# Two outlook-attention layers: the second layer's writes move to GpSimd's queue, its last softmax multiply to VectorE

## The chip, the cores and the metric

The kernel runs on one core of one Trainium2 chip. The time is the device time of one execution in microseconds, the median of three runs. A core has five engines with an instruction queue each, which run side by side and wait for one another through semaphores: TensorE (PE in the profile, its weight loads PEld), VectorE (DVE), ScalarE (ACT), GpSimd (POOL) and SyncE (SP, which only issues transfers). [...] An instruction that starts a transfer stands in its engine's queue like any other: if it has to wait for its data, what stands behind it waits too. Transfers of all queues are carried out by the same 16 DMA engines of the core.

## What is computed

The input is eight images of 56 x 56 pixels with 384 channels, in float32. Two layers follow each other, each of the form x + layer(groupnorm(x)).

```python
# layer 0: outlook attention with 12 heads, 9 x 9 weights a pixel and head
v = einsum(x, Wv);  a = softmax(einsum(x, Wa).reshape(b, n, 12, 9, 9) * d ** -0.5)
out = einsum('bnhpq,bnqhd->bnphd', a, patches3x3(v))   # then overlap-added over 3 x 3
y = einsum(canvas, Wo)
# layer 1: 6 heads, 9 weights a pixel and head
a = softmax((x @ W_attn + b_attn).reshape(B, H * W, 6, 9))
v = x @ W_v + b_v
y = einsum('bpKhd,bphK->bphd', patches3x3(v), a)
return y.reshape(B, H, W, C) @ W_proj + b_proj
```

In layer 1 each pixel's result is, for each head, the sum of the 3 x 3 neighbouring v vectors, weighted by nine softmax weights; a projection and the residual follow. The change touches layer 1 alone.

## The kernel before

The images are taken in four pairs, and one image column of a pair is R = 112 rows (two images of 56). Layer 0 goes through the 56 columns of each pair and leaves x1, the input of layer 1, in DRAM. Layer 1 goes through 32 groups (NG) of PX = 7 columns: four pairs times eight groups. It is a software pipeline written out in the loop over `step` at the end of `layer1`, with seven steps a group; parts of group g-1 are done while group g's projections run. TensorE's instructions are kept in program order, and the pieces of contraction and output projection are laid between the projections by a list of jobs (`jobs.run`). The order on the other engines is set by a scheduler that plans the whole program when it is built.

The parts of a group, in the order in which data goes through them:

- `load` (L798): SyncE reads x1t, the group's input, 1176 KB. `normed` (L813): ScalarE writes the normalized xn, in pieces for each channel chunk and image.
- `attend` (L842 to L858): TensorE projects a tile of 128 pixels (`bank`, L119 in the profile, where all matmuls have the line of a helper). VectorE adds the biases: the logits lgt (L852), and v (L855, five buffers). The two `spread` calls, L317 in the profile, then write v to the table vtab in DRAM, with the columns that belong to two groups written twice. Seven of eight steps have such a tile, and each tile has two writes, of parts of two columns.
- `regroup`: lgt is written to lgtab by ScalarE's queue (L869), and SyncE reads it back as `at`, one row of pixels a partition (L877).
- `weigh` (L886 to L897): the softmax. VectorE takes the maximum (L891) and subtracts it (L892), ScalarE takes the exponential (L893), VectorE sums (L895) and takes the reciprocal (L896); then the nine weights are multiplied by that (L897).
- `move`: TensorE shifts the weights between rows (`pw`), ScalarE copies them into bands wz in nine pieces (L918) and writes these to the table ztab in DRAM (L920), 496 KB in pieces of 504 bytes.
- `fetch`: SyncE reads the v patches vp from vtab (L378, after the v that they need has landed), and the bands z from ztab (L329, after ztab has landed), four transfers a group. TensorE contracts z with vp (`pc`), ScalarE copies the result to yT (L956), TensorE projects it (`po`), VectorE adds bias and residual into x1t (L972).
- `turn`: TensorE transposes the result (`pt`, L122), ScalarE copies it to ot (L985), and at the end of each half of a group ot is written to the output (L987): 64 writes in all, 672 KB and 504 KB in turn.

So before the change three queues hold transfers or wait for them in layer 1: ScalarE's, with 392 writes of v (L317), lgtab (L869) and ztab (L920) between its copies, exponentials and normalizations; SyncE's, with all reads and the writes of results; and GpSimd's, which issues no transfer and only multiplies the weights (L897).

Of the kernel before, what the change touches and what calls it, by code (L numbers as in the profile page):

```python
# [10 lines left out]
ALU = mybir.AluOpType  # L11
# [4 lines left out]
def two_outlook_layers(  # L16
# [32 lines left out]
    nc = tc.nc  # L49

    B, H, W, C = x.shape
# [33 lines left out]
    PY1, NPY1, SX1, SY1 = 8, 7, PX + 2, 10  # L85
# [25 lines left out]
    vtab1 = dram.tile([NPX * (R + GAP) + GAP, SX1, C], F32, name="vtab1")  # L111
# [6 lines left out]
    def matmul(*args, **kwargs):  # L118
        tc.keep_in_program_order(nc.tensor.matmul(*args, **kwargs))  # L119
# [23 lines left out]
    def projected(name):  # L143
        return patch.tile([P, NCH, PX, IMG, H], F32, tag="yT", name=f"yT_{name}", bufs=1)
# [146 lines left out]
    def project(dst, lhs, w, lo, n):  # L291
        for i in range(NCH):
            matmul(
                dst, lhs[:, i], w[:, i, lo : lo + n], start=(i == 0), stop=(i == NCH - 1)
            )

    def patches_of(col, pad):

        for px in range(NPX):
            sx = col - PX * px + pad  # L300
            if 0 <= sx < PX + 2 * pad:
                yield px, sx

    def parts_of(tile_no):


        done = OVER * tile_no
        yield 0, tile_no, done, R - done
        yield R - done, tile_no + 1, 0, done + OVER

    def spread(queue, table, width, col, pad, row, v):

        (px, sx), *more = patches_of(col, pad)
        n, rows = 1 + len(more), v.shape[0]
        line = width * C
        first = (px * (R + GAP) + GAP + row) * line + sx * C
        queue.dma_start(  # L317
            bass.AP(
                table.tensor, table.offset + first,
                [[line, rows], [(R + GAP) * line - PX * C, n], [1, C]],  # L320
            ),
            v.unsqueeze(1).to_broadcast([rows, n, C]),
        )
# [35 lines left out]
    def bank(rows, lo, hi, of=NBANK):  # L359

        bank.turn = (bank.turn + 1) % of
        return banks[bank.turn][:rows, lo:hi]
# [10 lines left out]
    def patch_tiles(name, b):  # L373
        return patch.tile([P, NPY0, C], F32, tag="vp", name=f"vp_{name}_{b}")

    def rows_to_patches(vp, table, px, r0, py, npy, sx):
        first = (px * (R + GAP) + GAP - MARGIN + r0) * sx * C
        nc.sync.dma_start(  # L378
            vp,
            bass.AP(  # L380
                table.tensor, table.offset + first, [[C, vp.shape[0]], [py * sx * C, npy], [1, C]]
            ),
        )
# [400 lines left out]
    def layer1(pools, base, last_of_layer0, late_w):  # L784
# [57 lines left out]
        def attend(g, m):  # L842

            col = g * PX + m
            if col % SB == 0:
                return
            tile_no = col % SB - 1
            tokens = xns[col // SB % 2].rearrange("p i m r -> p i (m r)")
            tokens = tokens[:, :, tile_no * P : (tile_no + 1) * P]
            pa = bank(P, 0, NC1, 2)  # L850
            project(pa, tokens, wc_t, 0, NC1)
            nc.vector.tensor_add(staged[-1][1][:, len(staged[-1][0])], pa[:, :NA1], ba_t)  # L852
            staged[-1][0].append(col // SB * NT + tile_no)
            v = work.tile([P, C], F32, tag="v", name=f"v_1_{col}", bufs=5)
            nc.vector.tensor_add(v, pa[:, NA1:], bv_t)  # L855
            for lo, n_col, row, n in parts_of(tile_no):
                c = col - col % SB + n_col
                spread(nc.scalar, vtab1, SX1, c % W, 1, row, v[lo : lo + n])  # L858

        def stage(g):  # L860

# [24 lines left out]
        def weigh(g):  # L886

            at = lgs[g]
            heads_last = [R, PX, K2, HEADS1]
            mx = work.tile([R, PX, HEADS1], F32, tag="mx", name=f"mx1_{g}")  # L890
            nc.vector.tensor_reduce(mx, at.rearrange("r x k h -> r x h k"), AX.X, ALU.max)  # L891
            nc.vector.tensor_tensor(at, at, mx.unsqueeze(2).to_broadcast(heads_last), ALU.subtract)  # L892
            nc.scalar.activation(at, at, AF.Exp)  # L893
            den = work.tile([R, PX, HEADS1], F32, tag="den", name=f"den1_{g}")
            nc.vector.tensor_reduce(den, at.rearrange("r x k h -> r x h k"), AX.X, ALU.add)  # L895
            nc.vector.reciprocal(den, den)  # L896
            nc.gpsimd.tensor_tensor(at, at, den.unsqueeze(2).to_broadcast(heads_last), ALU.mult)  # L897

        def move(g):

# [27 lines left out]
        def fetch(g, due):  # L928
            pair, px = divmod(g, NPX)
            n_tile = 2  # L930
            yT = projected(f"1_{g}")
            x1t = x1ts.pop(g)
            vps = [patch_tiles(f"1_{g}", b)[: SX1 * SY1, :NPY1] for b in range(IMG)]
            for b in range(IMG):
                rows_to_patches(vps[b], vtab1, px, b * H + MARGIN - 1, PY1, NPY1, SX1)
            for b in range(IMG):
                z, vp = zs1[(g * IMG + b) % NZ], vps[b]
                bands(
                    nc.sync, z, ztab1[g % NTAB], LINE1, SLOT1, ROW1, MARGIN - 1, GROUPS1,
                    b, PY1, NPY1,  # L940
                )

                def contract(t, b=b, z=z, vp=vp):
                    lo, hi = t * n_tile, min(NPY1, (t + 1) * n_tile)
                    pc = ps.tile([P, NCH, n_tile, PY1, PX], F32, tag="c", name=f"pc1_{g}_{b}_{t}", bufs=NC)
                    for py in range(lo, hi):
                        zp = z[:, py].rearrange("s (y h m) -> s y h m", y=PY1, h=HEADS1)
                        for h in range(HEADS1):
                            i, j = divmod(h, P // D1)
                            matmul(  # L950
                                pc[j * D1 : (j + 1) * D1, i, py - lo],
                                vp[:, py, h * D1 : (h + 1) * D1],
                                zp[:, :, h, :],
                                start=True, stop=True,
                            )
                    nc.scalar.copy(  # L956
                        yT[:, :, :, b, lo * PY1 : hi * PY1],
                        pc[:, :, : hi - lo].rearrange("p i n y m -> p i m (n y)"),
                    )

                for t in range(0, (NPY1 + n_tile - 1) // n_tile, NC):
                    jobs.add(due, lambda t=t, f=contract: [f(t + n) for n in range(NC)])

                    jobs.add(due, turning.pop(0) if turning else lambda: None)

            def project_out(half, j):
                lo, hi = HALVES[half]
                n = (hi - lo) * R
                po = ps.tile([P, 4 * R], F32, tag="of"[(half * NCH + j) % 2], name=f"po1_{g}_{half}_{j}")
                project_half(po, wo_t, yT, half, j)  # L970
                res = x1t[:, j, lo:hi].rearrange("p m r -> p (m r)")
                nc.vector.scalar_tensor_tensor(  # L972
                    res, po[:, :n], bo_t[:, j : j + 1], res, ALU.add, ALU.add
                )

            def turn(m):

                half = m // 4
                lo, hi = HALVES[half]
                if m == lo:  # L980
                    fetch.ot = io.tile([R, 4, C], F32, tag="ot", name=f"ot_{g}_{half}")
                pt = banks[-1][:R, :C] if m % 2 else ps.tile([R, C], F32, tag="t", name=f"pt1_{g}_{m}")
                for i in range(NCH):
                    transpose(pt[:, i * P : (i + 1) * P], x1t[:, i, m, :], ident)
                nc.scalar.copy(fetch.ot[:, m - lo, :], pt)  # L985
                if m == hi - 1:
                    nc.sync.dma_start(  # L987
                        of[pair * R : (pair + 1) * R, px * PX + lo : px * PX + hi, :],
                        fetch.ot[:, : hi - lo],
                    )  # L990

            out, back = project_out, turn
            for work_of in (
                (lambda: out(0, 0),), (lambda: out(0, 1),), (lambda: out(0, 2),),
                (lambda: out(1, 0), lambda: back(0)), (lambda: out(1, 1), lambda: back(1)),
                (lambda: out(1, 2), lambda: back(2)),
            ):
                jobs.add(due, lambda work_of=work_of: [w() for w in work_of])
            for m in range(3, PX):
                turning.append(lambda m=m: back(m))  # L1000
# [79 lines left out]
```

## Time and profile before

| | |
|---|---|
| time, median of three runs | 3550.35 us (3548.5 to 3552.01) |
| span of the profiled execution | 3569.5 us |
| mean granted TensorE clock | 0.982 |
| last multiply of layer 0 on GpSimd ends | about 2308 us |
| first projection of layer 1 | 2330.56 us |
| DMA, mean over the span | 235 GB/s |
| writes of v in layer 1: number, size, landing after issue | 392, 24 to 336 KB, most 3.6 to 7.6 us (medians by size) |
| multiply of the weights, L897 on GpSimd | 32, 943 ns each |

The page of a profile gives for each engine the time that it was busy and its share of the span. A line of a group of instructions reads: line, engine, operation, out<-in, count, busy time, mean duration, and then the idle time of that engine just before them, with what ended it. In a timeline each line has the start in us from the beginning of the span, the duration, the engine, the line of the kernel and the operation, then in brackets the idle time before it and what released it. "ACTq" and "SPq" are issues of transfers by ScalarE and SyncE: they hold the queue but do not count as busy. A line "A <- B: total, times, longest" of the waits view says how long A's engine stood idle until B. The windows view gives, for a stretch of the span, the busy time and (in brackets) the number of instructions of PE, PEld, DVE, ACT and POOL, then the granted TensorE clock as a share of full speed, the mean busy share of the DMA engines and GB/s.

### The profile page before, as it was taken

To read this page: it belongs to the slowest core of one execution; us is meant where nothing else is said; L and a number is where in the kernel's file an instruction comes from. 1 tells how busy PE (TensorE), PEld (TensorE's weight loads), DVE (VectorE), ACT (ScalarE), POOL (GpSimd) and SP (SyncE) were. 2 spreads that over 40 slices of the span, in tenths; PEclk is the share of its full clock that TensorE was granted. 3 is DMA by queue.
4 is the path that set the end of the run, shared out by engine and by line. 5 is a ranking of instruction groups with operands and counts; after the bars stand their busy time and mean duration, and the time that the engine had idled before them with its cause. 6 is when DMAs were issued, how large, how long until landed. Compare 5 with 4: busy or idle time off the path is not lost. (4 is left out here: it accounts for less than half of the span.)

```text
span 3569.5 us, 72083 instructions
## 1 busy us (share of the span) xinstructions
PE 3453.4 (97%) x29014; PEld 2365.3 (66%) x29014; DVE 1917.3 (54%) x4648; ACT 1165.0 (33%) x2727; POOL 984.5 (28%) x1409
## 2 busy tenths in 40 slices
PE   7899999999999999999999999989999999999998
PEld 5667767777777777777767767645565656556555
DVE  6666667667666676777666666532222222222322
ACT  4323233333333233333223323232333434334332
POOL 2543334344434434434434444310000000000000
PEclk8999999999999999999999999999999999999999
DMA  8999887688877778887667677677778787777876
GB/s 269 282 286 283 273 279 247 211 269 273 273 222 250 251 242 246 263 279 236 224 187 256 204 225 234 220 257 189 214 202 227 201 228 195 201 212 208 229 199 160
DMA packets 691452, 839.34 MB, mean 235 GB/s; under 512 B 302190, under 2 KB 595374, under 8 KB 687022
## 3 DMA queue, kind: packets, MB, share of 16 engines
q1 hardware_dynamic: 329614, 576.00, 50.9%
q10 hardware_dynamic: 361504, 258.73, 26.9%
q8 instruction: 228, 3.74, 0.5%
q14 instruction: 106, 0.87, 0.1%
HBM read 512.95 MB, written 321.66 MB: 234 GB/s over the span
## 5 line engine op out<-in xcount | busy, mean ns | idle before, releaser
L119 PE MATMUL bank<-wa_t,xn 128*112 128x288 f32 x4032 | 1087.3, 409 | 10.5 <-ACT v L562 6.8
L119 PEld LDWEIGHTS bank<-wa_t,xn 128*112 128x112 f32 x4032 | 693.8, 177 | 262.6 <-issue 34.6
L574 POOL TENSOR_TENSOR at<-at,den 112x972 f32<-112x972 f32 x224 | 504.6, 2253 | 1190.9 <-DVE den L573 1143.1
L119 PE MATMUL po<-yT,wo_t 128*128 128x448 f32 (+1 forms) x2304 | 820.6, 496 | 5.4 <-DVE x1t L685 4.8
L119 PEld LDWEIGHTS po<-yT,wo_t 128*128 128x128 f32 x2304 | 433.9, 191 | 294.7 <-issue 190.1
L119 PE MATMUL pc<-z,vp 121*32 121x49 f32 (+1 forms) x17664 | 491.9, 255 | 48.5 <-DMA z<-ztab 20.1
L119 PEld LDWEIGHTS pc<-z,vp 121*32 121x32 f32 (+1 forms) x17664 | 445.6, 132 | 125.5 <-issue 91.5
L119 PE MATMUL bank<-wc_t,xn 128*128 128x438 f32 x1176 | 495.6, 559 | 4.4 <-DMA wc_t<-in_wv 3.2
L550 DVE TENSOR_REDUCE mx<-bank 112x36 f32<-112x324 f32 x672 | 327.4, 487 | 307.3 <-PE bank L119 300.4
L119 PE MATMUL bank<-wv_t,xn 128*128 128x384 f32 x1176 | 419.2, 493 | 0.0
L897 POOL TENSOR_TENSOR at<-at,den 112x378 f32<-112x378 f32 x32 | 30.2, 943 | 1128.8 <-DVE den L896 925.1
L119 PEld LDWEIGHTS bank<-wc_t,xn 128*128 128x128 f32 x1176 | 220.1, 197 | 182.9 <-issue 172.1
L555 ACT ACTIVATE at<-at 112x972 f32<-112x972 f32 x224 | 227.0, 1014 | 349.4 <-DVE at L551 310.7
L551 DVE TENSOR_TENSOR at<-bank,mx 112x324 f32<-112x324 f32 x672 | 328.7, 489 | 21.1 <-DVE mx L550 0.5
L813 ACT ACTIVATE xn<-x1t,bias,scale 128x168 f32<-128x168 f32 (+4 forms) x498 | 213.7, 503 | 316.7 <-DMA x1t<-x 223.6
L119 PEld LDWEIGHTS bank<-wv_t,xn 128*128 128x128 f32 x1176 | 220.3, 191 | 140.0 <-issue 19.2
L972 DVE SCALAR_TENSOR_TENSOR x1t<-po,bo_t,x1t 128x448 f32<-128x448 f32 (+1 forms) x192 | 120.2, 626 | 324.1 <-PE po L119 324.1
L852 DVE TENSOR_TENSOR lgt<-bank,ba_t 128x54 f32<-128x54 f32 x196 | 41.4, 211 | 439.9 <-PE bank L119 439.9
L619 ACT COPY wt<-pw 112x120 f32<-112x120 f32 x224 | 58.1, 259 | 654.5 <-PE pw L119 573.6
L597 POOL TENSOR_TENSOR pre<-at,at 112x108 f32<-112x108 f32 (+1 forms) x440 | 237.1, 539 | 111.8 <-DVE wt L620 97.3
L567 DVE TENSOR_TENSOR d<-at 112x432 f32<-112x432 f32 x224 | 142.4, 636 | 204.3 <-ACT at L555 204.3
L664 ACT COPY yT<-pc 128x294 f32<-128x294 f32 x256 | 103.2, 407 | 373.6 <-PE pc L119 302.9
(92 smaller groups left out, 2806.8 us busy)
## 6 DMA issues: line engine op xcount, KB each, us to landing
z<-ztab SPq DMA_DIRECT2D x64, 2352.0 KB, 15.8
vp<-vtab SPq DMA_DIRECT2D x64, 1536.0 KB, 7.7
ztab<-wt ACTq DMA_DIRECT2D x336, 183.8 KB, 6.4
vp<-vtab SPq DMA_DIRECT2D x64, 945.0 KB, 9.7
xres<-xT SPq DMA_DIRECT2D x32, 1176.0 KB, 11.3
x1t<-x SPq DMA_DIRECT2D x32, 1176.0 KB, 9.5
xin<-xT ACTq DMA_DIRECT2D x54, 672.0 KB, 5.3
z<-ztab SPq DMA_DIRECT2D x128, 258.4 KB, 5.8
```

What stands on the lines that cost most here:

```text
L119: tc.keep_in_program_order(nc.tensor.matmul(*args, **kwargs))
L550: nc.vector.tensor_reduce(mx[:, pi, :], pl.rearrange("r q a -> r a q"), AX.X, ALU.max)
L551: nc.vector.tensor_tensor(at[:, pi], pl, mx[:, pi, :].unsqueeze(1).to_broadcast([R, K2, PH]), ALU.subtract)
L555: nc.scalar.activation(at, at, AF.Exp, scale=SCALE0)
L567: nc.vector.tensor_add(d4, at[:, :, 0:4], at[:, :, 4:8])
L574: nc.gpsimd.tensor_tensor(at, at, den.unsqueeze(2).to_broadcast([R, K, K2, PH]), ALU.mult)
L597: nc.gpsimd.tensor_tensor(dst, terms[0], terms[1], ALU.add)
L619: nc.scalar.copy(mid[:, 0 : E0 : E0 - 1, :], pw[:, 0 : E0 : E0 - 1, :])
L664: nc.scalar.copy(yT[:, :, :, b, rows_of], pc.rearrange("p i n y m -> p i m (n y)"))
L813: nc.scalar.activation(to[:, i, :, rows], x1ts[g][:, i, lo - first : hi - first, rows], AF.Identity, bias=bias[:, i, b : b + 1], scale=sca ...
L852: nc.vector.tensor_add(staged[-1][1][:, len(staged[-1][0])], pa[:, :NA1], ba_t)
L972: nc.vector.scalar_tensor_tensor(res, po[:, :n], bo_t[:, j : j + 1], res, ALU.add, ALU.add)
```

## The change

In layer 1 the writes of v and of the results are issued by GpSimd in place of ScalarE and SyncE, and VectorE multiplies the weights by the reciprocal of their denominators in place of GpSimd. GpSimd then has nothing else to do in layer 1 than these 456 writes, once it has cleared a few buffers when the layers change. It is meant to keep the waits that belong to these writes out of the two queues on which the path of a group depends, and to keep arithmetic from standing behind them on GpSimd.

```diff
             for lo, n_col, row, n in parts_of(tile_no):
                 c = col - col % SB + n_col
-                spread(nc.scalar, vtab1, SX1, c % W, 1, row, v[lo : lo + n])
+                spread(nc.gpsimd, vtab1, SX1, c % W, 1, row, v[lo : lo + n])
...
             nc.vector.reciprocal(den, den)
-            nc.gpsimd.tensor_tensor(at, at, den.unsqueeze(2).to_broadcast(heads_last), ALU.mult)
+            nc.vector.tensor_tensor(at, at, den.unsqueeze(2).to_broadcast(heads_last), ALU.mult)
...
                 if m == hi - 1:
-                    nc.sync.dma_start(
+                    nc.gpsimd.dma_start(
                         of[pair * R : (pair + 1) * R, px * PX + lo : px * PX + hi, :],
                         fetch.ot[:, : hi - lo],
                     )
```

The order of TensorE's instructions is the same in both kernels. On VectorE the multiply follows the reciprocal at once. On ScalarE and SyncE the moved issues are gone, and a few normalizations, copies and exponentials change places with their neighbours. On GpSimd the writes stand in the order of the columns, with a result's write between the writes of v.

## The prediction

> **What bounds the kernel now.** I read the page first, then the windows view to split the span by stage, then who TensorE waited for in the second stage, then the timelines of ScalarE and SyncE around single waits.
>
> ```profile
> PE 3453.4 (97%) x29014; PEld 2365.3 (66%) x29014; DVE 1917.3 (54%) x4648; ACT 1165.0 (33%) x2727; POOL 984.5 (28%) x1409
> 2500.00:2700.00 200.00, 190.57 (x1428) 119.35 (x1427) 55.31 (x120) 76.81 (x226) 4.73 (x5) 0.97 0.78 211
> ```
>
> TensorE is busy 97% of the span and sets the time. The changed lines run only in layer 1, from about 2330 us to the end (1240 us). In a window of it the columns are PE, weight loads, DVE, ACT, POOL, granted clock, DMA share, GB/s: GpSimd does five multiplies in 200 us, VectorE and ScalarE are under 40% busy, TensorE is idle 9.4 us of 200 and the mean granted clock is 0.97. So a change off TensorE can win only TensorE's idle time and the clock. The waits view for TensorE, 2300 to 3560 us (total us, times, longest):
>
> ```profile
> PE pc L119 <- DMA z<-ztab: 20.1, 11, 4.2
> PE pc L119 <- issue: 13.2, 7, 3.3
> PE pw L119 <- POOL at L897: 11.8, 8, 3.2
> PE pc L119 <- ACT yT L956: 5.3, 6, 1.8
> PE po L119 <- DVE x1t L685: 4.8, 7, 0.7
> ```
>
> The second line is the first under another name: those gaps too stand before the first pc of a group, 5 us after SyncE issued z. So z costs 33 us, the weights 12, yT 5, and the rest, layer change included, brings the sum to 65. Clock next, windows around two gaps:
>
> ```profile
> 2949.00:2962.00 13.00, 12.00 (x120) 7.96 (x118) 2.58 (x7) 5.20 (x13) 0.00 (x0) 1.00 0.51 120
> 2962.00:2975.00 13.00, 12.19 (x109) 8.43 (x110) 3.98 (x8) 4.32 (x11) 0.95 (x1) 0.74 0.83 225
> 3150.00:3180.00 30.00, 28.17 (x173) 16.97 (x171) 9.61 (x20) 10.37 (x33) 0.94 (x1) 1.00 0.86 240
> 3180.00:3192.00 12.00, 10.84 (x99) 7.29 (x100) 0.68 (x2) 2.96 (x8) 0.00 (x0) 0.72 0.37 78
> ```
>
> After the gap before 3181.16 (2.99 us, z) the clock falls to 0.72 for 12 us: 3.4 us of work lost on top. After a yT gap of 1.81 us near 2961 it falls to 0.74 for 13 us, again 3.4 us. A mean of 0.97 over 1240 us is some 37 us lost this way. At stake in layer 1 is therefore about 65 + 37 = 102 us, 2.9% of the kernel. Last, how ScalarE's issues of v enter (its timeline, two places):
>
> ```profile
> 2959.77 2.12 ACTq L317 DMA_DIRECT2D vtab<-v  x2
> 2961.93 0.48 ACT L985 COPY ot<-bank 112x384 f32<-112x384 f32 x1 [4.85 <-PE pt L122]
> 2962.31 0.64 ACT L956 COPY yT<-pc 128x336 f32<-128x336 f32 x2
> ...
> 3454.67 0.97 ACTq L317 DMA_DIRECT2D vtab<-v  x2
> 3455.68 0.99 ACT L918 COPY wz<-pw 112x42 f32<-112x42 f32 x9 [0.92 <-PE pw L119]
> 3456.71 0.32 ACTq L920 DMA_DIRECT2D ztab<-wz  x1
> ```
>
> First place: two issues of v hold ScalarE 2.12 us, the yT copies stand behind them, and that is the 1.81 us gap. Second: pw began at 3454.08, but wz is copied only when v has been issued, and ztab after that; then SyncE waits for ztab before it issues z:
>
> ```profile
> SPq L329 <- DMA ztab<-wz: 298.1, 32, 14.3
> ```
>
> That is 9.3 us a group: pw, wz, ztab, z, pc is the chain of a group, and TensorE's own work covers all but the last 1 to 3 us of it.
>
> [...]
>
> **The change part by part.**
> (a) The 32 multiplies move to VectorE. Each takes 0.55 us (L892) in place of 0.94, and the handing over goes (reciprocal ended 2711.94, GpSimd began 2712.17: 0.23). The weights come 0.62 us sooner. This counts in the 8 gaps before pw: -5 us, and perhaps one lowered stretch fewer, -2. VectorE gets 18 us more work, at 28% busy; behind the multiply stand the lgt and v sums, delayed 0.55 us with two banks to cover it: nothing.
> (b) 392 issues of v leave ScalarE. At 0.43 us each (a pair takes 0.8 to 1.0) that is 170 us, most of it in time when ScalarE had nothing else. On the path: the yT gaps, of 5.3 us I take 4 away, with two lowered stretches of 3.4 us less a little, 6: -10.
> (c) wz no longer stands behind v. Where v is in front, ztab is issued 2.4 to 2.6 us after pw begins, where it isn't, 1.96 (2713.17 to 2715.13): 0.5 us in the 18 z gaps, -9. And ztab no longer queues behind v's packets. The DMA view from 2715.1, where ztab was issued, to 2719.1:
>
> ```profile
> q1 hardware_dynamic: 533, 0.84, 85.3%
> q10 hardware_dynamic: 152, 0.20, 17.6%
> ```
>
> q10 (ScalarE) moved 0.20 MB in 152 packets, 1.3 KB each: v, not ztab's 504-byte pieces. Four us lost in this group; in most the first piece flows after 1 to 1.5 us. I take 0.5 us over the 18 gaps: -9. Against it [...] one v, 8 to 16 packets of 65 ns an engine, up to 1 us, I take 0.5: +9. [...] four stretches of 2.5 us, -10. Sum -19.
> (d) 64 result writes leave SyncE, where they waited 65 us in all for the copies (L987). The loads behind could go 0.7 us sooner (2713.23 to 2713.99 before x1t); nobody on the path waits for x1t alone, so nothing. On GpSimd v stands behind them; five v buffers, some 26 us of columns, hide that wait.
> (e) GpSimd's own issue is not in this trace. Low bound 0.43 us, ScalarE's[...]. I take 1 us. 456 transfers in 32 groups of 37 us are 14.3 a group, so 14 us[...]: GpSimd does not become the bound. But v lands later: +0.6 us for the pair's first, over 1 us for its second. Behind v stands vp on SyncE, behind vp x1t, behind x1t ScalarE's xn (0.5 us each, twelve), behind these the yT copies. At 2735.36 ScalarE waited 0.53 us for pc after that work, so about that much slack; I price the overrun at +8 (0 to 60).
> (f) Layer change: ScalarE spent 13.73 us on eight issues of v from 2335.40 with the last layer-0 copies behind them, -4; at the end a slower landing of the last result, +1.
> Sum: -7 -10 -19 +8 -4 +1 = -31: 3550.35 - 31 = 3519 us.
>
> **The rivals.** *Late v.* If a write of v lands 1.5 to 2 us later, x1t and ScalarE follow, less 0.5 us slack: 1 us more in 31 groups, and a lowered clock in a third of them at 3.4 us: 31 + 34 - 40 for the gains above = +25: 3575. For it: SyncE waits 157 us for v already (L378). Against: in the pair at 2743.09 the second piece was held over 1.5 us on ScalarE, so the new way may even be sooner. *Gaps close.* If z comes 2 us sooner everywhere, gaps and lowered clock mostly go: three quarters of 102, 3475. For: 14 of 18 z gaps are under 3 us. Against: ztab's 12 us are set by sharing the engines, and no byte is saved. *Nothing.* The sharing gives back what the issue saves, and only (a) remains, 3548. For: DMA share 0.78 throughout. Against: the 2.12 us above is plainly ScalarE's.
>
> **How the numbers follow.** Forecast, 3500 to 3543: 0.50. Gaps close, under 3500: 0.15. About nothing, 3543 to 3558: 0.14, of which 0.06 counts as faster. Late v, above: 0.21. Faster by over 0.2% (7 us): 0.50 + 0.15 + 0.06 = 0.71; same 0.08; slower 0.21. The range leaves one in ten on each side: 3478 to 3568, from near the closed gaps to most of late v.
>
> **What would show it.** Right: no L317 on ScalarE in layer 1, wz within 1 us of pw in every group, pw's wait for weights under 8 us, yT's gaps near nothing, z gaps under 25 us in sum, clock above 0.975 in layer 1, POOL issues near 1 us. Wrong: SyncE's wait for v (L378) growing well past 157 us with xn waiting longer for x1t, ztab landing later than before after its issue, or POOL issues over 2.6 us each, which would make GpSimd the bound.

## The result, and the profile after

The changed kernel takes 3609.58 us (median of 4 runs, 3595.99 to 3620.64) against 3551.18 us before (4 runs on the same chip, 3548.5 to 3559.18): ratio 1.0159, 95% interval 1.0119 to 1.0199. It is 58 us slower, where 31 us faster was forecast, and lies above the range of 3478 to 3568.

From the page of the changed kernel, and from its windows view (PE, weight loads, DVE, ACT, POOL, granted clock, DMA share, GB/s):

```profile
PE 3470.3 (96%) x29014; PEld 2370.8 (66%) x29014; DVE 1932.1 (53%) x4680; ACT 1174.1 (32%) x2727; POOL 1204.0 (33%) x1833
2500.00:2700.00 200.00, 185.16 (x1349) 113.70 (x1348) 55.34 (x119) 70.06 (x206) 39.02 (x72) 0.96 0.79 208
```

TensorE, busy 96% of the span, still sets the time, but in the same stretch of layer 1 it is idle 14.8 us of 200 in place of 9.4, at a clock of 0.96 in place of 0.97. DMA share and GB/s are close to those of before (0.78 and 211), so the transfers as a whole were not slowed. The waits view for TensorE from 2300 us on:

```profile
PE pw L119 <- DVE at L897: 47.3, 26, 3.9
PE pc L119 <- issue: 11.8, 7, 2.7
PE pc L119 <- DMA z<-ztab: 11.7, 6, 2.9
PE pc L119 <- ACT yT L956: 5.3, 3, 2.4
PE po L119 <- DVE x1t L685: 4.8, 7, 0.7
```

The waits for z fell from 33 us to 23, as hoped. The wait for the weights (pw, in front of which the softmax stands) rose from 11.8 us in 8 gaps to 47.3 in 26. VectorE is named, since its multiply came last, but the multiply takes 0.55 us and can't be a gap of up to 3.9. What VectorE itself waited for, first in the kernel before, then in the changed one:

```profile
DVE mx L891 <- DMA at<-lgtab: 84.5, 31, 7.6
```

```profile
DVE mx L891 <- DMA at<-lgtab: 156.3, 31, 9.6
```

VectorE's idle time before the softmax's first maximum, spent waiting for `at`, the read-back of the logits, is 72 us longer in all, or 2.3 us in each of 31 groups. The timeline around one such read, before (SyncE):

```profile
2706.14 0.31 SPq L877 DMA_DIRECT2D at<-lgtab  x1
2706.55 0.48 SPq L987 DMA_DIRECT2D out<-ot  x1
2707.20 5.93 SPq L378 DMA_DIRECT2D vp<-vtab  x2
```

and after (GpSimd, then SyncE, then VectorE):

```profile
2717.06 1.18 POOL L317 DMA_DIRECT2D vtab<-v  x2 [4.75 <-DVE v L855]
2718.23 0.56 POOL L987 DMA_DIRECT2D out<-ot  x1
...
2719.68 0.31 SPq L877 DMA_DIRECT2D at<-lgtab  x1
...
2724.76 0.83 DVE L891 TENSOR_REDUCE mx<-at 112x42 f32<-112x378 f32 x1 [4.08 <-DMA at<-lgtab]
```

Before, the write of the first half of the previous group's result (672 KB) stood in SyncE's queue right behind the read of `at` (165 KB). After, it is in a queue of its own and starts 1.5 us ahead of the read. From the read's issue to the maximum 5.1 us pass. What the 16 DMA engines did in that time is in the DMA view (packets, MB, share of the engines' time), here of the kernel before from 2706.14 to 2708.6:

```profile
q1 hardware_dynamic: 846, 0.45, 67.6%
q10 hardware_dynamic: 7, 0.00, 0.6%
```

and of the changed kernel from 2719.7 to 2724.8:

```profile
q0 software_dynamic: 201, 0.84, 55.5%
q1 hardware_dynamic: 941, 0.39, 33.3%
```

Before, SyncE's queue (q1) had the engines to itself while `at` was read; of its 0.45 MB the read is 0.17, the rest is the first part of the write behind it. After, GpSimd's (q0) took over half of their time: 0.84 MB in 201 packets, 4.2 KB each, against pieces of 216 bytes in the read. For its first 2.2 us after being issued the read moved nothing at all. The same view from 2719.7 to 2721.9 has no packet of q1:

```profile
q0 software_dynamic: 117, 0.60, 98.5%
```

In the mean of 29 groups the read's first piece starts 0.96 us after its issue before the change and 2.11 us after, and from the first piece to the end of the last 1.18 us pass before and 2.58 us after. So a later start and slower going share the loss. In this trace the two queues share the engines (55.5% and 33.3% of their time over the 5.1 us), but not in turns of one record of the view each: in those 2.2 us there were 117 of q0 and none of q1. What decides the order within was not tested. 672 KB at the 240 GB/s of that stretch is 2.9 us, and the read took 2.7 us longer up to the maximum (table below): about as if it had waited for the whole write. The changed kernel's own groups 1 and 31, in which no result write had been issued ahead of the read, took 2.46 and 2.55 us.

Where the 49 us between the two profiled spans (3569.5 and 3618.5) arose, from the times of the lgtab writes: up to the first one 1.4 us, between the third and the 31st 35.8, from there to TensorE's end 8.0, after TensorE's end 4.1. So it is 1.28 us for each group, and a longer end. Of the 1.28 us, 0.84 are idle time of TensorE (1.2 more before pw, 0.4 less before pc), and the other 0.44 are matmuls that run longer: between these two writes the mean granted clock was 0.964 in place of 0.972. The 2.7 us of the read are thus not passed on in full.

### The profile page after: what moved, and what is told of

The parts are those of the page before. It is cut to its first block, busy times and chain, and to the rows that moved or that the text cites. A ratio compares the mean times of both kernels' runs of the same rounds, so it can differ in the third digit from the quotient of the medians.

```text
span 3618.5 us, 72268 instructions
## 1 busy us (share of the span) xinstructions
PE 3470.3 (96%) x29014; PEld 2370.8 (66%) x29014; DVE 1932.1 (53%) x4680; ACT 1174.1 (32%) x2727; POOL 1204.0 (33%) x1833
## 5 line engine op out<-in xcount | busy, mean ns | idle before, releaser
L119 PE MATMUL po<-yT,wo_t 128*128 128x448 f32 (+1 forms) x2304 | 837.6, 504 | 5.3 <-DVE x1t L685 4.8
L119 PEld LDWEIGHTS po<-yT,wo_t 128*128 128x128 f32 x2304 | 441.3, 194 | 302.1 <-issue 199.6
L317 POOL DMA_DIRECT2D vtab<-v x392 | 213.4, 548 | 968.1 <-DVE v L855 950.0
L119 PE MATMUL pc<-z,vp 121*32 121x49 f32 (+1 forms) x17664 | 489.2, 255 | 35.8 <-issue 15.4
## 6 DMA issues: line engine op xcount, KB each, us to landing
xres<-xT SPq DMA_DIRECT2D x32, 1176.0 KB, 11.7
```

What stands on the lines that cost most here:

```text
L317: queue.dma_start(bass.AP(table.tensor, table.offset + first, [[line, rows], [(R + GAP) * line - PX * C, n], [1, C]],), v.unsqueeze(1).to_ ...
```

## The experiments

Four theories. R: the result write beside the at read. V: the writes of v on GpSimd's queue beside it. X: SyncE, rid of the results, issues x1t earlier, and ztab's pieces then stand behind it. M: the multiply in VectorE's queue. Each ratio is to the kernel before on the same chip. That kernel took 3571.13 us on the chip of the runs whose names begin with a, 3551.96 for b, 3578.19 for c1 and c2, 3586.37 for the last two, so times in us are compared within one chip only.

The table is worked out from the instruction and packet times in the traces, as means over groups 2 to 30 in us. "at read" is from its issue to the start of the first maximum, "first piece" from ztab's issue to its first 504-byte packet, "ztab to z" from issue to issue; pw and pc are TensorE's idle time just before a group's first one. The profiled execution of the kernel before was 0.5% above its median, that of the changed kernel 0.3% above, that of a3_m 0.3% below, so differences in period of 0.3 us mean little.

| kernel | at read | pw idle | first piece | ztab to z | pc idle | period | ratio to before, 95% interval |
|---|---|---|---|---|---|---|---|
| before | 2.56 | 0.26 | 2.13 | 11.94 | 0.98 | 37.14 | 1 |
| changed | 5.28 | 1.52 | 4.25 | 11.36 | 0.54 | 38.42 | 1.0159 (1.0119 to 1.0199) |
| a1_vm | 4.06 | 0.79 | 4.39 | 12.27 | 0.65 | 36.77 | 0.9994 (0.9980 to 1.0008) |
| a2_om | 5.16 | 1.69 | 4.29 | 10.59 | 0.32 | 38.44 | 1.0109 (1.0074 to 1.0144) |
| a3_m | 2.83 | 0.21 | 2.05 | 12.08 | 0.99 | 36.66 | 0.9985 (0.9968 to 1.0002) |
| a4_vo | 5.07 | 2.74 | 3.58 | 10.23 | 0.14 | 39.04 | 1.0191 (1.0155 to 1.0227) |
| b2_first | 4.39 | 1.20 | 3.50 | 10.51 | 0.12 | 38.35 | 1.0180 (1.0144 to 1.0217) |
| b3_second | 4.24 | 0.76 | 4.49 | 12.12 | 0.38 | 36.68 | 1.0019 (1.0007 to 1.0032) |
| b1_first_act | 4.66 | 1.14 | 4.47 | 11.70 | 0.66 | 37.87 | 1.0108 (1.0074 to 1.0143) |
| b4_hold | 2.66 | 0.13 | 3.97 | 12.64 | 0.48 | 36.42 | 1.0000 (0.9983 to 1.0017) |
| c2_hold_tail | 2.69 | 0.25 | 3.91 | 12.78 | 0.59 | 36.53 | 0.9949 (0.9931 to 0.9967) |
| c1_hold_vact | 2.80 | 0.22 | 4.73 | 11.62 | 0.44 | 36.69 | 0.9959 (0.9941 to 0.9978) |
| c2_again | 2.69 | 0.26 | 4.04 | 12.92 | 0.59 | 36.67 | 0.9959 (0.9944 to 0.9974) |
| d1_x1t_after | 2.77 | 0.27 | 1.52 | 13.10 | 0.62 | 36.92 | 0.9980 (0.9965 to 0.9994) |

### One part at a time

Four kernels, each with some of the three edits. **a1_vm**, against the changed kernel:

```diff
-                    nc.gpsimd.dma_start(   # results
+                    nc.sync.dma_start(
```

> Undoes one part: layer 1's v rows are written by GpSimd and the weights multiplied by VectorE, but both halves of the results stay on SyncE's queue. R (the result write beside the at read is the cause): at's read falls back from 5.3 us (issue to first reduction) to about 2.6 us, pw's idle time per group from 1.5 to about 0.3 us, the time to 3520-3550 us. V (v on GpSimd's queue is the cause): at's read stays near 5 us and the time at 3595-3620 us. X (SyncE's queue lets x1t pass ahead of ztab): the first ztab packet comes again about 2.1 us after its issue instead of 4.2; some half of the loss goes, 3565-3590 us.

**a2_om**, against the changed kernel:

```diff
-                spread(nc.gpsimd, vtab1, SX1, c % W, 1, row, v[lo : lo + n])
+                spread(nc.scalar, vtab1, SX1, c % W, 1, row, v[lo : lo + n])
```

> Results written by GpSimd and weights multiplied by VectorE; v stays on ScalarE's queue. R: at's read near 5 us, pw idle 1.2-1.5 us per group, 3590-3620 us. V: at's read near 2.6 us, 3540-3560 us. X: at's read near 2.6 us but ztab's first packet still about 4 us after its issue, 3565-3590 us.

**a3_m** has both of these edits, and so only the multiply of the change:

> Only the multiply moves from GpSimd to VectorE. R, V and X all leave this unharmed: at's read 2.6 us, from the softmax's last step to pw 0.4 us instead of 0.9, time 3540-3550 us (-5 to -10 us on before). If the multiply itself were the cause (VectorE's queue), 3590 us or more.

**a4_vo**, against the changed kernel:

```diff
-            nc.vector.tensor_tensor(at, at, den.unsqueeze(2).to_broadcast(heads_last), ALU.mult)
+            nc.gpsimd.tensor_tensor(at, at, den.unsqueeze(2).to_broadcast(heads_last), ALU.mult)
```

> v and results by GpSimd, but the multiply stays on GpSimd behind those issues. R and V both: at's read near 5 us, and the multiply now waits behind an issue of 0.55 us or behind a result write that waits for its projection, so 3600-3660 us. If the multiply on VectorE were the cause, it would be near 3550 us.

Taking the results off GpSimd removes the loss (a1: 0.9994), taking v off leaves most of it (a2: 1.0109). On this chip a2 and a3 differ by the results alone: 0.0124 of 3571 us, 44 us. V and M fall as main causes. X can't be it either: in a1 ztab's first piece comes as late as in the changed kernel (4.39 us) without a loss. a4 shows what the multiply's move is worth once GpSimd issues writes: there the multiply starts 0.74 us after the reciprocal's end in the mean, in place of 0.22 before the change, and pw's idle time nearly doubles.

a1 missed one number of R: at's read fell to 4.06 us, not to 2.6. SyncE's timeline of a1 says why:

```profile
2704.72 0.34 SPq L987 DMA_DIRECT2D out<-ot  x1
2707.41 0.31 SPq L877 DMA_DIRECT2D at<-lgtab  x1
```

The scheduler, planning ScalarE without the issues of v, put the result in front of the read in 26 of the 29 groups. The read then stands behind the write in one queue. It loses less than in the changed kernel, but here the write also has the longer lead, 2.6 us in the median against 1.4 in the mean. a1 loses nothing in sum although its read is 1.5 us longer than before: pw's idle time grew by 0.5 us a group and pc's fell by 0.3. It is the idle time of both together that goes with the loss: 1.2 to 1.4 us a group in before, a1 and a3, 2.0 to 2.9 in the changed kernel, a2 and a4.

### Which half, and which queue

**b2_first** and **b3_second** leave one half of the results on GpSimd; **b1_first_act** tries another foreign queue for the first half:

```diff
-                    nc.gpsimd.dma_start(
+                    (nc.sync if half else nc.gpsimd).dma_start(   # b2_first
+                    (nc.gpsimd if half else nc.sync).dma_start(   # b3_second
+                    (nc.sync if half else nc.scalar).dma_start(   # b1_first_act
```

> The changed kernel, but only the first half of each group's result (four windows, 672 KB) is written by GpSimd; the second half is back on SyncE. R (the first half's write runs beside the at read): at's read stays near 5 us, pw's idle time near 1.3 us per group, time 1.2 to 1.7% above before. If the second half were the cause: at's read below 4 us and the time within 0.4% of before.

> The reverse: first half on SyncE, second half by GpSimd. R: at's read 2.6 to 4 us (4 where SyncE's queue puts the write ahead of the read), time within 0.4% of before. If the second half were the cause (it meets ztab and x1t): 1% or more above before.

> First half written from ScalarE's queue, second half from SyncE's; v and the multiply as in the changed kernel. Tells whether GpSimd's kind of queue matters or any queue other than SyncE's does the harm. Any other queue: at's read near 5 us and the time 1.2% or more above before. GpSimd's queue alone [...]: at's read below 4 us and the time within 0.5% of before.

The first half carries nearly all of it: 1.0180 against 1.0019 on the same chip, 57 us. b2 has a cost of its own in this, though. Its waits view for TensorE and SyncE's timeline of one group show it:

```profile
PE bank L119 <- ACT xn L813: 20.1, 5, 5.7
```

```profile
2544.60 1.96 SPq L329 DMA_DIRECT2D z<-ztab  x4
2546.68 0.35 SPq L798 DMA_DIRECT2D x1t<-x  x1
```

In b2 the scheduler put the next x1t behind z on SyncE in 7 of 29 groups; the normalized xn then came late, and TensorE waited 20.1 us for it, against 1.2 in the changed kernel. That leaves some 37 of the 57 us for the write beside the read. The second half is written some 11 us after at's issue; b3, which has it on GpSimd, is 0.2% above before. b3's at read, 4.24 us, is slightly above what was expected, again with the first half ahead of the read on SyncE. From ScalarE's queue the first half costs 1.08%, 38 us: so in these runs it is mainly that the queue is another one, not whose it is. DMA view of b1_first_act during such a read, 2711.6 to 2715.8:

```profile
q0 software_dynamic: 170, 0.51, 38.7%
q10 hardware_dynamic: 73, 0.35, 29.4%
q1 hardware_dynamic: 800, 0.17, 18.9%
```

There the result goes out on q10, in packets of 4.8 KB, the v on q0, and the read of `at` on q1 is left with 18.9% of the engines. b2 stands 0.7% above b1, 26 us, and the 20 us for xn, a wait that is 1.2 us in b1, account for most of that; so these runs do not show that GpSimd's queue is dearer.

### The same writes, later

**b4_hold** is the changed kernel, but the first half waits in GpSimd until the maximum of the next softmax, and so the read of `at`, is through; the value added is zero:

```diff
+            flush(mx)              # in weigh, behind the maximum: issues the held write
...
+    nc.gpsimd.tensor_tensor(zero, mx[0:1, 0, 0:1], mx[0:1, 0, 0:1], ALU.subtract)
+    nc.gpsimd.tensor_tensor(ot[0:1, 0, 0:1], ot[0:1, 0, 0:1], zero, ALU.add)
     nc.gpsimd.dma_start(of[...], ot[:, : hi - lo])
```

> The changed kernel with one thing added: GpSimd issues the first half only after the at read has landed (two 1x1 operations on GpSimd tie the write to the first maximum; the number added to the result is zero). R: at's read falls to 2.6 to 3.5 us, pw's idle time to at most 0.5 us per group, time 0 to 0.6% below before, with GpSimd still writing all v and all results. If the harm is from GpSimd's queue as such, or from SyncE letting x1t pass: the time stays 1% or more above before.

Its timeline (SyncE, VectorE, GpSimd):

```profile
2703.89 0.31 SPq L877 DMA_DIRECT2D at<-lgtab  x1
...
2706.43 0.86 DVE L896 TENSOR_REDUCE mx<-at 112x42 f32<-112x378 f32 x1 [1.21 <-DMA at<-lgtab]
...
2708.56 0.56 POOL L1001 DMA_DIRECT2D out<-ot  x1 [0.37 <-POOL ot L1000]
```

and its DMA view from 2703.9 to 2706.6:

```profile
q1 hardware_dynamic: 819, 0.20, 46.2%
q0 software_dynamic: 50, 0.16, 18.1%
```

The read is back at 2.66 us, and pw's idle time at 0.13 us a group is lower than before the change. GpSimd still writes all v (two v writes were issued 2.3 us before this read) and all results. With the same queues, bytes and instructions apart from the tie, the loss is gone: it is the overlap in time. R stands. The time is at the edge of what was expected, no gain over before. Nor is the later write free: TensorE waits 11.7 us in 8 gaps for copies into ot before its transposes, 2.9 in the changed kernel. Before the longest of them, which ends at 3460.26 us, the copy stood behind normalizations that had waited for x1t, and ScalarE's wait for x1t is 316 us in place of 250. Whether the held write delays x1t was not tested.

**c2_hold_tail** puts the last group's two writes back on SyncE, since GpSimd's last write landed late; **c1_hold_vact** is the same with v on ScalarE:

```diff
-                        nc.gpsimd.dma_start(
+                        (nc.sync if g == NG - 1 else nc.gpsimd).dma_start(
```

> b4_hold, and the last group's two writes go back to SyncE without the hold. The period of the groups stays at b4's 36.4 us (before: 37.1), and the end after TensorE's last instruction falls from 9.8 to about 5.7 us: some 4 us under b4_hold, 0.1 to 0.5% below before. If the tail were not GpSimd's own: no change against b4_hold.

> c2_hold_tail with v back on ScalarE: asks what moving v is worth once the result write no longer meets the at read. If v on GpSimd helps (the prediction's parts b and c): 5 to 20 us slower than c2_hold_tail, with z's idle time per group back near 1 us. If it does nothing or costs: the same time or less.

The end after TensorE's last instruction fell from 9.8 to 5.7 us as expected, and c2 is faster than before by 0.5%, again by 0.4% in c2_again. By the ratios it beats the changed kernel too. The 4 us at the end are 0.1%; b4 ran on another chip, and how much of the rest of its distance to c2 is the chip is open. c1 is no slower than c2 beyond the intervals: with the overlap gone, moving v has no effect that these runs can tell, and z's idle time did not return to 1 us, as it should have if v's move had shortened it. What c2 and c1 share against before is the multiply and the held results; which of the two brings how much was not separated on one chip.

### x1t behind ztab

**d1_x1t_after**, against c2_hold_tail:

```diff
+                nc.gpsimd.tensor_copy(t[0:1, 0, 0:1], wzs[g % 2][0:1, last : last + 1])
                 nc.sync.dma_start(t, x1s[pair][px])
```

> c2_hold_tail with one more tie: the load of the next group's x1t is issued only after the last copy into wz (a 1x1 copy on GpSimd that the load overwrites), so that the ztab write no longer stands behind it. X (x1t ahead of ztab is what ate the gain that the prediction's part c hoped for): the first ztab packet comes 1 to 2 us after its issue instead of 3.9, ztab to z shortens by 1.5 to 2.5 us, z's idle time per group goes from 0.6 to about 0.2 us, and the time falls 5 to 15 us below c2_hold_tail. If ztab is only delayed by other traffic, or the later x1t holds the normalization up instead: the same time as c2_hold_tail or more.

> c2_hold_tail once more, as the base of d1_x1t_after on the same chip: 0.3 to 0.7% below before.

ztab's first piece came at 1.52 in place of 4.04 us, and nothing was won: ztab to z took 13.10 in place of 12.92 us, and the ratio is 0.2% above c2's, with overlapping intervals. An explanation that fits, but is not shown, is that ztab and x1t are in flight together either way and the order of their starts does not change the sum. The tie also puts a further wait into GpSimd's queue, whose price was not measured apart.

## Why the prediction was wrong

The step that failed is (d): "nobody on the path waits for x1t alone, so nothing". It asked who stands *behind* the result writes in SyncE's queue, and priced the move by that. It did not ask what the position in that queue did for the transfer in *front*: the write stood behind the read of `at`, and its first piece started 0.8 us after the read's first (means of 29 groups). On GpSimd it is issued when its copy is done, 1.1 to 2.5 us ahead of the read, and its first piece starts 2.1 us before the read's first; at's read grows by 2.7 us a group in the mean. Measured price of the step: 44 us (a2 against a3); b1 gives 38 us for the first half alone, b2 against b3 57 us, 20 of them by another wait. Step (c) had reckoned with a sharing of the engines for v beside ztab, +9, an estimate; step (d) did not.

- (a), the multiply, -7: a3 alone gave -5 us (0.0015 of 3571; the interval reaches 1.0002). Right in size, though a3 can't tell it from nothing. That nothing behind it on VectorE suffers fits a3, which lost nothing.
- (b), yT gaps, -10: 5.3 us before, 5.3 us after, so not seen in the changed kernel.
- (c), z, -19: the idle time before z fell by 10 us (33 to 23), near the two terms of -9 less the +9. That is luck, in good part: with v still on ScalarE and only results and multiply moved (a2), pc's idle time is 0.32 us a group against 0.99 in a3, and 0.44 in c1, so moving the results shortens the wait for z too, which (d) had put at nothing; v's move alone (a1) gives 0.65. The -10 for the clock, the author's estimate, did not come: in layer 1 (2400 to 3500 us) the clock went from 0.97 to 0.96. Nor does the trace before show one size of gap under which the clock holds: 1.4 us after the end of a gap of 1.15 us (at 3005.7) the clock fell to 0.50 and stayed there for 3.4 us, and it did not fall after one of 1.82 us (at 3105.7). wz did begin earlier (1.13 us after pw in place of 1.41), but "ztab no longer queues behind v's packets" was mis-sized: the first piece came 2.1 us later, behind x1t, and d1 shows that even undoing this wins nothing.
- (b) and (c) together, -29: with the overlap gone, c2 against c1 gives -0.1% by the ratios, within the intervals, and +1.4 us by the medians. These terms were far too large.
- (e), +8: GpSimd's issues took 0.55 us, below the 1 us assumed, which was the author's estimate, and SyncE's wait for v fell from 156.6 to 135.6 us. No overrun was seen, and the rival *Late v*, which had the time's direction right, is not what happened.
- (f), -4 +1: the first lgtab write of layer 1 stands at 2367.2 us, before at 2365.8, so the -4 isn't there, and the landing of the last result took 4.1 us more, not 1.

```profile
L317 POOL DMA_DIRECT2D vtab<-v x392 | 213.4, 548 | 968.1 <-DVE v L855 950.0
```

This row of the changed kernel's page is (e)'s price: 548 ns an issue. Of the signs named, the wait of pw for weights ("under 8 us") was the one that told: it read 47.3. None of the signs of failure named the read of `at`.

## What to carry to other kernels

Here two transfers in one queue were also an order: before the change the write's first piece started 0.8 us after the read's first, and from GpSimd's queue 2.1 us before it. Before moving a large write to an idle engine's queue, list the small reads on a short chain that stood in front of it, and price the read as if the whole write went through first: bytes over the measured GB/s, here an estimate of 2.9 us for 672 KB, with 2.7 measured. That is one size of write on one kernel; and it is the delay of the read, of which the group passed on 1.28 us. If the engine is to have the write all the same, tie its issue to the landing of that read; here the tie brought the ratio back to 1.0000, though TensorE got a new wait before its transposes. And compare the order of every queue after an edit: in a1 and b2 the scheduler had swapped transfers that the edit did not name.

## What was not expected of the hardware

- With the 672 KB write issued ahead of it, the 165 KB read in pieces of 216 bytes took longer up to the maximum, whether the write was in another queue or in its own: 5.28 us in the changed kernel (another queue, 1.4 us ahead), 4.06 us in a1 (the same queue, mostly 2.6 us ahead), 2.56 us with the write behind it. The lead differs between the first two by about as much as the read, so they do not say which arrangement is dearer.
- In d1_x1t_after an earlier start did not bring an earlier end: ztab's first piece came 2.5 us sooner after its issue than in c2_again (1.52 and 4.04 us), and the issue of z, which waits for ztab's landing, 0.2 us later (13.10 and 12.92 us).
- An issue on GpSimd held that engine for 548 ns in the mean, little more than the 486 ns that ScalarE took in the mean for the same writes before the change (median 437).
